# Int8 product of a post-norm decoder moved, in steps, between the quads of its second cross attention

## Chip, core and metric

The kernel runs as one program on one NeuronCore of a Trainium2 chip. The metric is the device time of one execution in microseconds (us). It was run three times, and one more execution was recorded by the hardware profiler. PE is the tensor engine, DVE the vector engine, ACT the scalar engine, POOL the GpSimd engine, and SP the engine that issues most DMAs.

## What is computed

Sixteen sequences of 100 tokens with 256 channels pass through two decoder layers. Each sublayer is followed by an addition and a layernorm. The change touches the last two sublayers only, which are, cut to what matters:

```python
# second cross attention: 16 heads of 64, context of 361 rows with 192 channels
q, k, v = x @ Wq, context @ Wk, context @ Wv
attn = softmax(q @ k.T / 8)
x = layernorm(x + attn @ v @ Wo + bo)

# int8 product with a 256 x 256 right side
lhs_scale = max(abs(x), axis=channels) / 127          # one for each token
rhs_scale = max(abs(rhs), axis=rows) / 127            # one for each column
q_lhs = clip(round(x / lhs_scale), -127, 127)
q_rhs = clip(round(rhs / rhs_scale), -127, 127)
out = layernorm(x + (q_lhs @ q_rhs) * lhs_scale * rhs_scale)
```

The rounded values are whole numbers up to 127 and are held as bf16 for the matmul; the rest of the kernel computes in fp32.

## The kernel before

The 16 sequences stand in four groups of four (`G = 4`, `NG = 4`); `self.x[g]` is a tile of 100 tokens x 4 sequences x 256 channels. The sublayers run one after the other. The last two are the function `cross1` and, behind it in a pool of its own, `quantize_rhs` and four calls of `int8_product`, each followed by the DMA of its group to the output (L1807 to L1811).

**The second cross attention** goes over 64 quads: quad n handles four of the 16 heads of sequence b = n // 4. `attend` (L544) writes the order of PE, ACT and DVE by hand; POOL and SP are ordered by the planner from the order of the program. For each n it issues, in this order:

- `scores(b, quad)`: four score products on PE into two double PSUM banks (L1634), two reduces for the row maximum on DVE (`top`, L1639), four exponentials with row sums on ACT (L1644);
- interleaved, `prepare(b + 1, quad)` and `values` of quad n - 2. The first projects keys (PE L599 and L601, copied out by DVE as `k`, L1598) and, in quads 1 to 3 of a sequence, sources (copied out by DVE as `v`, L1615). The second transposes the probabilities on PE in three tiles (L608), copies them out (`pT`, L611, the first tile on DVE, the other two on ACT), multiplies them by the sources (PE L1673) and copies the result out on ACT (`oT`, L1679);
- `weigh(b, quad)`: a reciprocal of the row sums on DVE (`den`, L1652) and, on POOL, the product of the probabilities with it (L1653);
- at two quads behind the last one of a sequence, so at n % 4 == 1, `finish(b)`: the output projection on PE (16 instructions of L155) and the addition to the residual row on DVE (L1690). For the last sequence of a group, `finish` also calls `close` (L539): the whole layernorm of four sequences, that is eight short DVE instructions for the statistics (L185, L186), a square root on ACT (L192), a reciprocal (L198) and four normalizing instructions on DVE (L200).

`attend` has a parameter `done`, whose steps would go to later quads; `cross1` doesn't use it. PE, ACT and DVE each work through their instructions strictly in this order. PSUM tiles come from three rings of two buffers: `tr` for everything transposed and for the value products, `mm` for projections, `sc` for the scores. An engine that wants a buffer waits until the tile two places earlier in that ring is read out.

**The int8 stage** is not ordered by hand. `quantize_rhs` (L1697) loads the right side, transposes it, takes the scales (L1735 to L1737), rounds by adding and subtracting a large constant (L1715, L1716), clips, turns it back as bf16 and spreads the column scales over the tokens with a matmul (L1725). `int8_product` (L1740) does the like for one group: maximum, scale and inverse (L1735 to L1737), four times scale and round (L1745), two clips over the whole tile (L1748, L1750), eight bf16 transposes (L1755) with two copies on ACT (L1758), eight bf16 matmuls (L155), four times the two scales on DVE (L1770), the addition of x on POOL (L1774) and a layernorm.

Of the kernel before, what the change touches and what calls it, by code (L numbers as in the profile page):

```python
# [90 lines left out]
class Net:  # L91
# [449 lines left out]
        self.x[g] = r  # L541


    def attend(self, scores, prepare, values, finish, queries, weigh, depth, done=lambda g: []):  # L544

        n_quads = 4 * B
        engines = {mybir.EngineType.PE, mybir.EngineType.Activation, mybir.EngineType.DVE}
        with self.tc.manual_schedule(engines=engines):  # L550
            queries(0)
            for part in range(4):
                for step in prepare(0, part):
                    step()
            later = {}
            for n in range(n_quads + depth):
                b, quad = divmod(n, 4)
                ahead, behind = [], []
# [4 lines left out]
                if n >= depth:  # L563
                    behind = values(*divmod(n - depth, 4))
                for i in range(max(len(ahead), len(behind))):
                    for steps in (ahead, behind):
                        if i < len(steps):
                            steps[i]()
                if n < n_quads:
                    weigh(b, quad)  # L570
                if n < n_quads and quad == 2 and b % G == G - 1 and b + 1 < B:
                    queries(b // G + 1)
                for step in later.pop(n, []):
                    step()
                if n >= depth and (n - depth) % 4 == 3:
                    b = (n - depth) // 4
                    finish(b)
                    if b % G == G - 1:

                        for i, step in enumerate(done(b // G)):  # L580
                            later.setdefault(n + 2 * i + 2, []).append(step)
            for n in sorted(later):
                for step in later[n]:
                    step()

    def load_context(self, pool, b):
# [973 lines left out]
    def cross1(self, pool):  # L1560
# [3 lines left out]

        def queries(g):
            x = self.x[g]
            xT = pool.tile([P, 2, GT], F32, tag="xT", name="xT")
            self.transposed(x, xT)

            qTs[g] = []  # L1570
            for i in range(8):
                pq = self.ps("mm")
                self.mm(
                    pq[:, :GT],
                    [(self.x1["wq"][:, k, i * P : (i + 1) * P], xT[:, k, :]) for k in range(2)],
                )
# [120 lines left out]
    def quantize_rhs(self, pool):  # L1697

        nc, small = self.nc, self.small
        raw = pool.tile([P, 2, C], F32, tag="rhs_raw", bufs=1, name="rhs_raw")  # L1700
        nc.sync.dma_start(raw, self.a["rhs"].rearrange("(k p) n -> p k n", p=P))
        self.ident16 = pool.tile([P, P], BF16, tag="ident16", bufs=1, name="ident16")
        nc.vector.tensor_copy(self.ident16, self.c("ident"))
        self.rhs_q = pool.tile([P, 2, C], BF16, tag="rhs_q", bufs=1, name="rhs_q")
        self.rhs_s = pool.tile([T, C], F32, tag="rhs_s", bufs=1, name="rhs_s")
        ps_s = self.ps("mm")
        for o in range(2):
# [10 lines left out]
            nc.vector.tensor_scalar(q16, q, -127.0, None, ALU.max)  # L1718
            pb = self.psum.tile([P, 2, P], BF16, tag="tr", name="tr16")
# [3 lines left out]
            wide = pool.tile([P, T], F32, tag="rhs_wide", bufs=1, name="rhs_wide")  # L1723
            nc.vector.tensor_scalar(wide, self.ones[:, :T], scale, None, ALU.mult)
            nc.tensor.matmul(  # L1725
                ps_s[:T, o * P : (o + 1) * P], wide, self.c("ident"), start=True, stop=True
            )
        nc.scalar.copy(self.rhs_s, ps_s[:T, :C])

    def scales(self, src, rows, n):  # L1730

# [5 lines left out]
        nc.vector.reciprocal(inv, scale)  # L1737
        return scale, inv

    def int8_product(self, pool, g):  # L1740
        nc, x = self.nc, self.x[g]
        scale, inv = self.scales(x, T, G)
        q = pool.tile([T, G, C], F32, tag="q", name="q")
        for b in range(G):
            nc.vector.tensor_scalar(  # L1745
                q[:, b, :], x[:, b, :], inv[:, b : b + 1], MAGIC, ALU.mult, ALU.add
            )
        nc.vector.tensor_scalar(q, q, MAGIC, 127.0, ALU.subtract, ALU.min)  # L1748
        q16 = pool.tile([T, G, C], BF16, tag="q16", name="q16")
        nc.vector.tensor_scalar(q16, q, -127.0, None, ALU.max)  # L1750
        qT = pool.tile([P, 2, GT], BF16, tag="qT16", name="qT16")
        for k in range(2):
            pt = self.psum.tile([P, G, T], BF16, tag="tr", name="tr16")
            for b in range(G):
                nc.tensor.transpose(  # L1755
                    pt[:, b, :], q16[:, b, k * P : (k + 1) * P], self.ident16[:T, :T]
                )
            nc.scalar.copy(qT[:, k, :].rearrange("p (b t) -> p b t", b=G), pt)  # L1758
        r = self.xp.tile([T, G, C], F32, tag="x", name="r")
        for h in range(2):  # L1760
            po = self.ps("mm")
            for b in range(2):
                at = (2 * h + b) * T
                self.mm(
                    po[:T, b * C : (b + 1) * C],
                    [(qT[:, k, at : at + T], self.rhs_q[:, k, :]) for k in range(2)],
                )
            for b in range(2):
                bb = 2 * h + b
                nc.vector.scalar_tensor_tensor(  # L1770
                    r[:, bb, :], po[:T, b * C : (b + 1) * C], scale[:, bb : bb + 1], self.rhs_s,
                    ALU.mult, ALU.mult,
                )
        nc.gpsimd.tensor_tensor(r, r, x, ALU.add)  # L1774
        self.layernorm(r)
        self.x[g] = r


@with_exitstack
def tile_decoder(ctx: ExitStack, tc: tile.TileContext, a: dict, out: bass.AP):  # L1780
# [17 lines left out]
    with tc.tile_pool(name="w_x1", bufs=1, side="right") as wp:  # L1798
        with tc.tile_pool(name="w_out", bufs=1) as w_out:
            net.load_mamba_out(w_out)  # L1800
            net.load_cross1(wp)
            with tc.tile_pool(name="mamba", bufs=2) as pool:
                net.mamba(pool)
        w_in.release()
        with tc.tile_pool(name="cross1", bufs=2) as pool:
            net.cross1(pool)
# [144 lines left out]
```

## Time and profile before

| what | us |
|---|---|
| three runs, median (lowest to highest) | 2077.32 (2067.65 to 2079.21) |
| the profiled execution, its own time | 2075.14 |
| its span, from the first to the last instruction | 2073.4 |
| PE busy over the span | 1813.3 |
| DVE busy over the span | 1120.9 |
| ACT busy over the span | 961.7 |
| POOL busy over the span | 690.1 |
| mean granted clock of PE over the span | 0.932 |
| the row of the last sequence is added (L1690) from | 2015.57 |
| last normalizing instruction of the kernel ends | 2068.1 |

How to read the views: the page of a profile divides the span into 40 slices, 51.8 us each, with the busy share of each engine in tenths. The windows view gives busy time in stretches that one chooses: stretch, its length, then for PE, weight loads (PEld), DVE, ACT and POOL the busy time and the number of instructions, then the granted PE clock (1.00 is full), the share of the DMA engines and GB/s. The timeline lists single instructions: start, duration, engine, line, operation, output and inputs, shapes, and in brackets the idle time of that engine just before and what ended it. "x4" stands for four instructions put together. Matmuls of fp32 count as two instructions each.

### The profile page before, as it was taken

What the parts mean: (1) busy time and instruction counts of PE and PEld (TensorE: products, weight loads), DVE (VectorE), ACT (ScalarE), POOL (GpSimd) and SP (SyncE); (2) the same over time, 40 slices, a digit from 0 to 9 for tenths busy, and PEclk for the clock granted to TensorE, in tenths of its full rate; (3) what the DMA queues carried; (4) which work ended last, traced back from release to release, by engine and by line L of the source; (5) the groups of instructions that cost most, each with busy time, mean ns of one, the idle gap of its engine ahead of it and who ended that gap; (6) DMA issues with size and microseconds to landing.
All of it is one profiled execution on the core that took longest, in us unless ns stands there. A gap on an engine that the chain in (4) does not pass through costs nothing. (4 is left out here: it accounts for less than half of the span.)

```text
span 2073.4 us, 31998 instructions
## 1 busy us (share of the span) xinstructions
PE 1813.3 (87%) x12268; PEld 1066.0 (51%) x12268; DVE 1120.9 (54%) x2458; ACT 961.7 (46%) x2266; POOL 690.1 (33%) x501
## 2 busy tenths in 40 slices
PE   6997999999939994699798899899999999999972
PEld 3565555555626663355455555445545554555551
DVE  3445576667632222587878867444344434434437
ACT  4552476667512221476676676333343334333341
POOL 2222232324320002366667566422223222322221
PEclk9999999999769998699999999999999999999995
DMA  4700600101051114211111111000000000000001
GB/s 130 312 1 1 222 23 16 33 22 32 6 177 44 46 43 143 66 51 53 45 46 60 44 51 38 15 16 8 8 8 15 8 8 8 16 8 8 1 6 32
DMA packets 46840, 96.99 MB, mean 47 GB/s; under 512 B 5835, under 2 KB 25931, under 8 KB 44257
## 3 DMA queue, kind: packets, MB, share of 16 engines
q1 hardware_dynamic: 41632, 83.75, 11.9%
q0 software_dynamic: 5056, 11.20, 1.8%
q8 instruction: 98, 1.61, 0.3%
q14 instruction: 54, 0.43, 0.1%
HBM read 69.48 MB, written 25.44 MB: 46 GB/s over the span
## 5 line engine op out<-in xcount | busy, mean ns | idle before, releaser
L1653 POOL TENSOR_TENSOR s<-s,den 100x1444 f32<-100x1444 f32 x64 | 165.9, 2593 | 513.3 <-DVE den L1652 513.3
L155 PE MATMUL mm<-xT,w_mamba_in 128*128 128x400 f32 x512 | 205.1, 545 | 31.0 <-ACT sz L1344 27.6
L1644 ACT ACTIVATE s<-sc,top 100x361 f32<-100x361 f32 x256 | 140.2, 560 | 158.4 <-DVE top L1639 158.3
L1639 DVE TENSOR_REDUCE top<-sc 100x2 f32<-100x722 f32 x128 | 110.4, 903 | 131.2 <-PE sc L1634 131.2
L611 ACT COPY pT<-tr 128x400 f32<-128x400 f32 (+1 forms) x192 | 94.0, 492 | 182.0 <-PE tr L608 181.8
L753 ACT ACTIVATE w_experts<-w_experts,top 100x361 f32<-100x361 f32 x256 | 149.3, 586 | 41.3 <-POOL w_experts L745 41.1
L1195 DVE SCALAR_TENSOR_TENSOR xc<-mm,pv,xc 128x388 f32<-128x388 f32 (+2 forms) x192 | 119.9, 624 | 80.6 <-ACT xc L1190 75.7
L745 POOL TENSOR_SCALAR w_experts<-w_experts 100x1444 f32<-100x1444 f32 x64 | 88.8, 1388 | 223.1 <-DVE w_experts L741 154.8
L155 PEld LDWEIGHTS mm<-xT,w_mamba_in 128*128 128x128 f32 x512 | 100.7, 205 | 116.0 <-ACT sz L1344 35.2
L611 DVE COPY pT<-tr 128x400 f32<-128x400 f32 x192 | 105.1, 568 | 99.7 <-PE tr L608 66.7
L741 DVE TENSOR_SCALAR_CACHE_REDUCE w_experts<-sc 100x361 f32<-100x361 f32 x256 | 121.0, 528 | 10.6 <-PE sc L735 9.0
L1615 DVE COPY v<-mm 128x512 f32<-128x512 f32 (+1 forms) x96 | 61.8, 686 | 112.2 <-PE mm L601 112.2
L608 PE MATMUL tr<-cn,w_experts 100*128 100x100 f32 (+1 forms) x768 | 101.4, 270 | 21.1 <-ACT pT L611 12.4
L155 PE MATMUL sc<-w_experts,e_xT 128*128 x256 | 117.6, 603 | 2.1 <-DMA e_x<-rows 2.1
L608 PEld LDWEIGHTS tr<-cn,s 100*128 100x128 f32 (+1 forms) x768 | 74.7, 151 | 84.4 <-issue 66.2
L1378 POOL TENSOR_TENSOR y<-y,sz 128x400 f32<-128x400 f32 x64 | 66.4, 1038 | 143.4 <-DVE y L1375 112.4
L608 PE MATMUL tr<-cn,s 100*128 100x100 f32 (+1 forms) x768 | 97.8, 263 | 13.4 <-DVE pT L611 13.4
L1315 POOL TENSOR_TENSOR L<-L,cols 100x800 f32<-100x800 f32 x64 | 99.9, 1561 | 26.3 <-DMA L<-sums 26.3
L599 PE MATMUL mm<-x_wv,ctx 128*128 128x512 f32 (+1 forms) x192 | 96.1, 624 | 9.2 <-DVE k L1598 9.2
L1144 POOL DMA_INDIRECT e_sum<-rows,slots x32 | 33.0, 1031 | 213.6 <-DMA x_wq<-in_x_wo_dram 204.3
L1598 DVE COPY k<-mm 128x361 f32<-128x361 f32 x128 | 62.4, 529 | 76.4 <-PE mm L601 76.4
L1398 PE MATMUL acc<-y,w_mamba_out 128*128 128x400 f32 x256 | 102.6, 524 | 0.0
(297 smaller groups left out, 3691.3 us busy)
## 6 DMA issues: line engine op xcount, KB each, us to landing
L<-sums SPq DMA_DIRECT2D x64, 312.5 KB
rows<-nothing SPq DMA_DIRECT2D x15, 1024.0 KB
w_experts<-in_moe_w_dram SPq DMA_DIRECT2D x24, 512.0 KB
ctx<-in_ctxT_dram SPq DMA_DIRECT2D x32, 361.0 KB
e_x<-rows SPq DMA_DIRECT2D x32, 128.0 KB
rows<-e_y SPq DMA_DIRECT2D x32, 128.0 KB
w_mamba_in<-in_m_w_in_dram SPq DMA_DIRECT2D x1, 2048.0 KB
w_mamba_in<-in_m_w_in_dram POOLq DMA_DIRECT2D x1, 2048.0 KB, 9.9
```

The costliest lines, as they stand in the source:

```text
L155: self.nc.tensor.matmul(out, lhsT, rhs, start=i == 0, stop=i == len(pairs) - 1)
L599: self.nc.tensor.matmul(out, lhsT, rhs, start=True, stop=False)
L608: self.nc.tensor.transpose(pt[:n, h * T : (h + 1) * T], probs[:, h, k0 : k0 + n], self.ident(T))
L611: evict(pT[:n, k, :], pt[:n, :GT])
L741: nc.vector.tensor_scalar(s[:, h, :], sc[h // 2][:T, h % 2, :CTX], -1e4, 1e4, ALU.max, ALU.min, accum_out=top[:, h : h + 1],)
L753: nc.scalar.activation(s[:, h, :], s[:, h, :], AF.Exp, bias=top[:, h : h + 1], scale=-1.0, accum_out=dens[b][:, hd : hd + 1],)
L1195: nc.vector.scalar_tensor_tensor(a3[:, :, s:], p3[:, :, : T - s], w(k), a3[:, :, s:], ALU.mult, ALU.add)
L1315: nc.gpsimd.tensor_tensor(ls[n], ls[n], bc(c, 3, T), ALU.subtract)
L1398: nc.tensor.matmul(acc[:, c, :GT], self.w_out[:, i, c * P : (c + 1) * P], y, start=i == 0, stop=i == 15)
L1639: nc.vector.tensor_reduce(top[:, 2 * p : 2 * p + 2], sc[p][:T, :, :CTX], AX.X, ALU.max, negate=True)
L1644: nc.scalar.activation(s[:, h, :], sc[h // 2][:T, h % 2, :CTX], AF.Exp, bias=top[:, h : h + 1], accum_out=den[:, h : h + 1],)
L1653: nc.gpsimd.tensor_tensor(s, s, bc(den, 2, CTX), ALU.mult)
```

## The change

The int8 product becomes a list of small steps, and `attend` issues them at the ends of quads. `attend` takes a table `later` from quad number to steps in place of `done`; a step of quad n comes after everything else of quad n, `finish` included, and quads go on after the 66th with nothing but such steps.

- `close` is no longer called from `finish`. Two steps take its place: `means` (statistics and square root) and `normal` (reciprocal and normalizing), one quad apart.
- For groups 0 to 2 the list begins one quad behind the `finish` of the group's last sequence, at n = 18, 34 and 50 (all n % 4 == 2), with one step in each quad: `means`, `normal`, `steps_of` (scales, and rounding L1745), `bounded` (the two clips), `turned(0)`, `turned(1)` (four transposes and a copy each), two `product` steps (four matmuls and two DVE instructions each), `plus` (POOL), `means`, `normal` with the DMA to the output. That is eleven quads.
- The last group is closed in two parts: sequences 12 to 14 from n = 62, and sequence 15 from n = 66. From n = 66 on, both lists have a step at the same n, and that of the first part is issued first.
- `quantize_rhs` becomes four steps, issued in quads 4 to 7. Its load is issued ahead of the attention, and its tiles and those of the product now lie in the pool of the cross attention, in one buffer each; `xT` of the queries has one buffer there instead of two. The spread of the column scales goes through the `tr` ring, in two halves.

Its core:

```diff
-            later = {}
-            for n in range(n_quads + depth):
+            for n in range(max(n_quads + depth, max(later) + 1)):
...
-                for step in later.pop(n, []):
-                    step()
-                if n >= depth and (n - depth) % 4 == 3:
-                    b = (n - depth) // 4
-                    finish(b)
-                    if b % G == G - 1:
-                        for i, step in enumerate(done(b // G)):
-                            later.setdefault(n + 2 * i + 2, []).append(step)
+                if depth <= n < n_quads + depth and (n - depth) % 4 == 3:
+                    finish((n - depth) // 4)
+                for step in later.get(n, []):
                     step()
...
-            xT = pool.tile([P, 2, GT], F32, tag="xT", name="xT")
+            xT = pool.tile([P, 2, GT], F32, tag="xT", bufs=1, name="xT")
...
-            if b % G == G - 1:
-                self.close(rs[g], g)
-        self.attend(scores, prepare, values, finish, queries, weigh, 2)
+        def means(g, bs):
+            mvs[g] = self.means(rs[g], bs)
+            mvs[g] = mvs[g], self.deviations(mvs[g], bs)
+        def normal(g, bs):
+            self.normalize(rs[g], *mvs.pop(g), bs=bs)
+            self.x[g] = rs[g]
+        for i, step in enumerate(self.quantize_rhs(pool)):
+            add(4 + i, step)
+        for g in range(NG):
+            for bs in [(0, 1, 2, 3)] if g + 1 < NG else [(0, 1, 2), (3,)]:
+                n = 4 * (g * G + bs[-1]) + 6
+                steps = [lambda g=g, bs=bs: means(g, bs), lambda g=g, bs=bs: normal(g, bs)]
+                steps += self.int8_product(pool, g, bs, q_rs)
+                for i, step in enumerate(steps):
+                    add(n + i, step)
+        self.attend(scores, prepare, values, finish, queries, weigh, 2, later)
...
+        return [
+            lambda: steps_of(self.x[g]), bounded, lambda: turned(0), lambda: turned(1),
+            *[lambda two=two: product(two) for two in (bs[:2], bs[2:]) if two],
+            plus, means, normal,
+        ]
...
-    with tc.tile_pool(name="int8", bufs=2) as pool:
-        net.quantize_rhs(pool)
-        for g in range(NG):
-            net.int8_product(pool, g)
-            nc.sync.dma_start(out[g * G : (g + 1) * G].rearrange("b t c -> t b c"), net.x[g])
```

The arithmetic of each step is the one described above, cut to the sequences `bs` that it is called for.

More of the change, by code (lines that the diff above doesn't have):

```diff
@@ L541, in close, with attend @@
         self.x[g] = r
-    def attend(self, scores, prepare, values, finish, queries, weigh, depth, done=lambda g: []):
+    def attend(self, scores, prepare, values, finish, queries, weigh, depth, later):
         n_quads = 4 * B
@@ L562, in attend @@
                         ahead = prepare(b + 1, quad)
-                if n >= depth:
+                if depth <= n < n_quads + depth:
                     behind = values(*divmod(n - depth, 4))
@@ L572, in attend @@
                     queries(b // G + 1)
-                for step in later.pop(n, []):
-                    step()
-                if n >= depth and (n - depth) % 4 == 3:
-                    b = (n - depth) // 4
-                    finish(b)
-                    if b % G == G - 1:
-                        for i, step in enumerate(done(b // G)):
-                            later.setdefault(n + 2 * i + 2, []).append(step)
-            for n in sorted(later):
-                for step in later[n]:
+                if depth <= n < n_quads + depth and (n - depth) % 4 == 3:
+                    finish((n - depth) // 4)
+                for step in later.get(n, []):
                     step()
@@ L1690, in finish @@
             nc.vector.tensor_tensor(row, po[:T, :C], row, ALU.add)
-            if b % G == G - 1:
-                self.close(rs[g], g)
-        self.attend(scores, prepare, values, finish, queries, weigh, 2)
+        mvs, q_rs = {}, {}
+        def means(g, bs):
[4 more added lines that the diff above has]
+            self.x[g] = rs[g]
+        later = {}
+        add = lambda n, step: later.setdefault(n, []).append(step)
+        for i, step in enumerate(self.quantize_rhs(pool)):
[8 more added lines that the diff above has]
+        self.attend(scores, prepare, values, finish, queries, weigh, 2, later)
     def quantize_rhs(self, pool):
@@ L1702, in quantize_rhs, with quantized @@
         self.ident16 = pool.tile([P, P], BF16, tag="ident16", bufs=1, name="ident16")
-        nc.vector.tensor_copy(self.ident16, self.c("ident"))
         self.rhs_q = pool.tile([P, 2, C], BF16, tag="rhs_q", bufs=1, name="rhs_q")
         self.rhs_s = pool.tile([T, C], F32, tag="rhs_s", bufs=1, name="rhs_s")
-        ps_s = self.ps("mm")
-        for o in range(2):
+        d = {}
+        def quantized(o):
+            if o == 0:
+                nc.vector.tensor_copy(self.ident16, self.c("ident"))
             pt = self.ps("tr")
@@ L1718, in quantize_rhs, with turned @@
             nc.vector.tensor_scalar(q16, q, -127.0, None, ALU.max)
+            wide = pool.tile([P, T], F32, tag="rhs_wide", bufs=1, name="rhs_wide")
+            nc.vector.tensor_scalar(wide, self.ones[:, :T], scale, None, ALU.mult)
+            d[o] = q16, wide
+        def turned(o):
+            q16, wide = d.pop(o)
             pb = self.psum.tile([P, 2, P], BF16, tag="tr", name="tr16")
@@ L1722, in quantize_rhs @@
             nc.scalar.copy(self.rhs_q[:, :, o * P : (o + 1) * P], pb)
[L1723 to L1728, printed above, removed]
+            pw = self.ps("tr")
+            nc.tensor.matmul(pw[:T, :P], wide, self.c("ident"), start=True, stop=True)
+            nc.scalar.copy(self.rhs_s[:, o * P : (o + 1) * P], pw[:T, :P])
+        return [lambda f=f, o=o: f(o) for o in range(2) for f in (quantized, turned)]
     def scales(self, src, rows, n):
@@ L1738, in scales @@
         return scale, inv
[L1740 to L1746, printed above, removed]
-            )
[L1748 to L1756, printed above, removed]
-                )
[L1758 to L1769, printed above, removed]
@@ new lines, in int8_product, with steps_of, bounded, turned @@
+    def int8_product(self, pool, g, bs, rs):
+        nc, nb = self.nc, len(bs)
+        at, cols = slice(bs[0], bs[-1] + 1), slice(bs[0] * T, (bs[-1] + 1) * T)
+        d = {}
+        def steps_of(x):
+            d["scale"], inv = self.scales(x[:, at], T, nb)
+            q = d["q"] = pool.tile([T, G, C], F32, tag="q8", bufs=1, name="q8")
+            for i, b in enumerate(bs):
+                nc.vector.tensor_scalar(
+                    q[:, b, :], x[:, b, :], inv[:, i : i + 1], MAGIC, ALU.mult, ALU.add
+                )
+        def bounded():
+            q = d["q"]
+            nc.vector.tensor_scalar(q[:, at], q[:, at], MAGIC, 127.0, ALU.subtract, ALU.min)
+            d["q16"] = pool.tile([T, G, C], BF16, tag="q16", bufs=1, name="q16")
+            nc.vector.tensor_scalar(d["q16"][:, at], q[:, at], -127.0, None, ALU.max)
+        def turned(k):
+            if k == 0:
+                d["qT"] = pool.tile([P, 2, GT], BF16, tag="qT16", bufs=1, name="qT16")
+            pt = self.psum.tile([P, G, T], BF16, tag="tr", name="tr16")
+            for b in bs:
+                nc.tensor.transpose(
+                    pt[:, b, :], d["q16"][:, b, k * P : (k + 1) * P], self.ident16[:T, :T]
+                )
+            nc.scalar.copy(
+                d["qT"][:, k, cols].rearrange("p (b t) -> p b t", b=nb), pt[:, at]
+            )
+        def product(two):
+            if two[0] == 0:
+                rs[g] = self.xp.tile([T, G, C], F32, tag="x", name="r")
+            po, r = self.ps("mm"), rs[g]
+            for i, b in enumerate(two):
+                self.mm(
+                    po[:T, i * C : (i + 1) * C],
+                    [(d["qT"][:, k, b * T : (b + 1) * T], self.rhs_q[:, k, :]) for k in range(2)],
+                )
+            for i, b in enumerate(two):
+                j = b - bs[0]
@@ L1770, in int8_product, with plus @@
                 nc.vector.scalar_tensor_tensor(
-                    r[:, bb, :], po[:T, b * C : (b + 1) * C], scale[:, bb : bb + 1], self.rhs_s,
+                    r[:, b, :], po[:T, i * C : (i + 1) * C], d["scale"][:, j : j + 1], self.rhs_s,
                     ALU.mult, ALU.mult,
                 )
-        nc.gpsimd.tensor_tensor(r, r, x, ALU.add)
-        self.layernorm(r)
-        self.x[g] = r
+        def plus():
+            r = rs[g]
+            nc.gpsimd.tensor_tensor(r[:, at], r[:, at], self.x[g][:, at], ALU.add)
@@ new lines, in means, with normal @@
+        def means():
+            mv = self.means(rs[g], bs)
+            d["mv"] = mv, self.deviations(mv, bs)
+        def normal():
+            r = rs[g]
+            self.normalize(r, *d["mv"], bs=bs)
+            b0 = g * G
+            nc.sync.dma_start(
+                self.out[b0 + bs[0] : b0 + bs[-1] + 1].rearrange("b t c -> t b c"), r[:, at]
+            )
+        return [
[3 more added lines that the diff above has]
+        ]
@@ L1805, in tile_decoder @@
         with tc.tile_pool(name="cross1", bufs=2) as pool:
+            net.out = out
             net.cross1(pool)
-    with tc.tile_pool(name="int8", bufs=2) as pool:
-        net.quantize_rhs(pool)
-        for g in range(NG):
-            net.int8_product(pool, g)
-            nc.sync.dma_start(out[g * G : (g + 1) * G].rearrange("b t c -> t b c"), net.x[g])
     net.psum.release()
```

## The prediction

> **What bounds the kernel now.** First the windows view: a plain sequence of four quads, one in which a group is closed, the end of the attention, and the stretch from the last residual row to the end.
>
> ```profile
> 1573.79:1612.57 38.78, 37.72 (x250) 20.62 (x249) 17.35 (x31) 14.36 (x44) 10.37 (x5) 1.00 0.04 10
> ...
> 1702.20:1745.07 42.87, 39.58 (x250) 20.99 (x249) 20.72 (x44) 17.11 (x47) 10.37 (x5) 0.96 0.03 9
> ...
> 1989.97:2015.99 26.02, 21.57 (x193) 15.34 (x192) 6.76 (x13) 10.99 (x30) 6.46 (x3) 1.00 0.00 1
> 2015.99:2073.40 57.41, 14.01 (x76) 9.31 (x76) 45.96 (x133) 6.15 (x16) 10.04 (x4) 0.54 0.12 34
> ```
>
> A plain sequence is bound by PE (37.72 of 38.78 us); DVE is busy for 17.35 us. The last stretch, 57.4 us, is bound by DVE (45.96), and PE does 14.01 at half clock. The change spreads most of that DVE work over stretches where DVE has room. A closing costs 42.87 - 38.78 = 4.09 now; the timeline tells how:
>
> ```profile
> 1709.00 1.38 DVE L200 TENSOR_SCALAR x_row<-x_row,ln_mv,ln_rstd 100x256 f32<-100x256 f32 x4
> ...
> 1710.30 1.72 DVE L1639 TENSOR_REDUCE top<-sc 100x2 f32<-100x722 f32 x2
> 1711.28 1.28 ACT L1644 ACT_TABLE_LOAD   x1 [2.52 <-DVE top L1639]
> 1711.94 0.96 DVE L1598 COPY k<-mm 128x361 f32<-128x361 f32 x2
> 1712.51 0.30 PEld L599 LDWEIGHTS mm<-x_wv,ctx 128*128 128x128 f32 x2 [2.43 <-DVE k L1598]
> 1712.51 3.06 PE L599 MATMUL mm<-x_wv,ctx 128*128 128x512 f32 x4 [2.24 <-DVE k L1598]
> 1712.57 0.56 ACT L1644 ACTIVATE s<-sc,top 100x361 f32<-100x361 f32 x1
> ```
>
> The layernorm stands before `top` on DVE, so `k` is late and PE waits 2.24. The other 1.85 is the clock: after the wait it was 0.66 for 4 us, and the sources took 3.06 instead of 1.93. So DVE's slack where one quad ends and the next begins (call it a seam) is what counts. Timeline, a plain seam:
>
> ```profile
> 1585.93 0.17 DVE L1652 RECIPROCAL den<-den 100x4 f32<-100x4 f32 x1
> 1586.24 2.59 POOL L1653 TENSOR_TENSOR s<-s,den 100x1444 f32<-100x1444 f32 x1 [10.35 <-DVE den L1652]
> ...
> 1587.56 1.73 DVE L1639 TENSOR_REDUCE top<-sc 100x2 f32<-100x722 f32 x2 [1.46 <-PE sc L1634]
> ...
> 1590.37 0.98 DVE L1598 COPY k<-mm 128x361 f32<-128x361 f32 x2 [1.08 <-PE mm L601]
> ```
>
> A step lands between `den` and `top`. DVE idles 1.46 there and 1.08 before `k`: 2.5 us are free, and each further one holds PE. After the first quad of a sequence (n % 4 == 0) it is 2.91 + 1.08 = 4.0; after `finish` (n % 4 == 1) 0.37 + 1.08 = 1.45. But POOL starts its 2.59 right after `den`. What that does to DVE, in the last stretch (a tiny instruction, normally 0.14) and as the attention starts:
>
> ```profile
> 2034.10 2.72 POOL L1774 TENSOR_TENSOR r<-r,x_row 100x1024 f32<-100x1024 f32 x1 [27.50 <-DVE r L1770]
> 2034.53 2.31 DVE L1736 TENSOR_SCALAR q_scale<-q_scale 100x4 f32<-100x4 f32 x1
> ```
>
> ```profile
> 1321.35 0.39 DVE L185 BATCH_NORM_STATS2 ln_st<-r 100x6 f32<-100x256 f32 x1
> ...
> 1323.07 3.14 DVE L200 TENSOR_SCALAR r<-r,ln_mv,ln_rstd 100x256 f32<-100x256 f32 x4
> ```
>
> A TENSOR_SCALAR from SBUF to SBUF is held until POOL is done (3.14 instead of 1.38 beside POOL's L207, 1320.43 to 1325.09); the statistics are not (0.39 beside it), nor is `top`, which reads PSUM.
>
> **The change, part by part.** Sums are made against the profiled span of 2073.4; the execution took 2075.14, 1.7 more and 2.2 below the median of the three runs.
>
> *Tail, -36.4.* The old one, from the end of the last L1690 (2015.99), is 57.4. The new one, with that end as zero: clips of three sequences, 2 x 0.68 x 3/4 = 1.0; transposes and copy (0.53 + 0.50, three of four sequences) to 1.9; ACT then loads the square root table for sequence 15 (1.28 + 0.30) before the second copy: 4.0; first product 1.0, two L1770 of 0.42: 5.8; sequence 15's scales (1.1) stand before the third L1770: 7.3; POOL 2.34 x 3/4: 9.1; a clip of 0.3 held by it and statistics 3 x 0.55: 11.1; root, reciprocal, three L200: 12.7. Then sequence 15: its L1770 13.1, POOL 0.6, statistics 0.55, root 0.4, reciprocal and L200 0.5: 15.4; output and end as now, 2073.4 - 2068.1 = 5.3: 20.7, say 21. 57.4 - 21 = 36.4. Both ends: if every second wait overlaps better 18, if each POOL and table wait doubles 26.
>
> *Groups 0 to 2, +2.3 each, +6.9.*
> - The closing leaves `finish`: -4.09.
> - PE work: 8 transposes (0.85) and 8 matmuls (1.94) at clock 0.50; at 1.00 half of it: +1.4. All on the path, as PE is the bound.
> - `means` (n % 4 == 2): 2.21 of statistics from `den`, under 2.5: 0. ACT loads two tables more (1.28 each); exponentials come 2.0 late, but in a quad with sources the second `pT` copy (1591.26) is needed only when the value products start (1594.43): 3 to spare.
> - `normal` (n % 4 == 3): L200 is held by POOL until 2.6 after `den`, then 1.0 to 1.4: ends 3.9 after it, 1.4 over 2.5. +1.4; with PE's usual 0.7 gap there it is a gap like the 2.24 above, so +1.5 for clock (bounds 0 and 1.85).
> - `steps_of` (n % 4 == 0): reduce 1.21, L1736 held until POOL ends, reciprocal, four L1745 of 0.33: 0.5 over. The trace has no such reduce beside POOL; bounds 0 (not held, nothing late) and 1.7 (held); I take 0.5, as the statistics of the nearest row were not held.
> - `bounded`, after `finish`: POOL is idle by then, 1.3 against 1.45: 0. `turned`, `product`: DVE's two L1770 read PSUM, ACT's copy (0.45) fits its 1.46 of idle: 0 beyond PE. `plus`: POOL has 5 us idle in each quad: 0; without that cover the probabilities, due two quads later, still come in time. The outputs go through SP between loads of contexts that are issued once in four quads: 0.
> - second `means` (n % 4 == 3): exponentials 2.0 late (0.75 from `top`, 1.28 table) before a quad without sources, where the copies (1600.54 for products at 1601.69) have only 1.0 with ACT's own idle 0.42: +1.0, and +0.5 for clock. second `normal`: +0.1.
> - Sum: 1.4 + 1.4 + 1.5 + 0.5 + 1.0 + 0.5 + 0.1 - 4.09 = 2.3.
>
> The Trainium skill, "ScalarE: Activation LUTs", section "What ACT_TABLE_LOAD costs", puts a drain of 1.38 behind each load of 1.28 and so speaks against four loads in place of two. The row above differs: the exponential starts 1.29 after its load. By the page the second `means` would cost 1.4 more in each group, 4 us in all; I go by the row.
>
> The Trainium skill, "SBUF — State Buffer", section "Who interferes with whom", says that a `tensor_reduce` never contends with GpSimd on this chip. By it `steps_of` keeps its 0.5; were the reduce held, the sum would be 3.6 higher. No run here shows it yet.
>
> *Right side, quads 4 to 7, +4.1.* PE work L1710, L1721, L1725, 3.06 in the tail at mostly half clock: +1.7. At n = 4 DVE ends 0.35 over; at n = 6 L1736 waits for POOL and the rest takes 1.6 more: 1.55 over; clock +0.5. The load, now early on SP, is due 36 us after the attention starts; xT's single buffer is free since the group before: 0. Bounds 1.7 and 7.3.
>
> *Last group inside the loop, +4.0.* From n = 62 no projections run and the quads hang on the chain score, `top`, exponential, copy (5.86 each, 1993.53 to 1999.39). `means` at 62 puts a table load into it: +1.4. `normal` at 63 waits for POOL ahead of a `pT` copy: +1.75. Clock +0.85. `steps_of` ends 0.3 before the next `pT`: 0; without that cover up to 1.
>
> Sum: -36.4 + 6.9 + 4.1 + 4.0 = -21.4: span 2052.0, time 2053.7, so **2054 us**.
>
> **Rivals.**
> - *Steps hide.* DVE's TENSOR_SCALARs get in ahead of POOL (0.14 lies between the end of `den` and POOL's start). Then a group costs 1.4 + 1.0 + 0.5 - 4.09 = -1.2, the right side 1.7, the last group 1.4: -36.4 - 3.6 + 3.1 = -36.9, time **2038**. Against it: L1736 at 2034.53 was held although other DVE work preceded it. 0.2.
> - *Every stall drops the clock.* 1.85 for `normal`, `means` and `steps_of` of each group: 5.8 a group, 17.4; right side 7.3, last group 6.9: -36.4 + 31.6 = -4.8, time **2070**, within 0.5%. Against it: quads with gaps of 0.87 and 0.84 (2002.6 and 2004.0) ran at 1.00; for it: like gaps at 1980.5 and 1981.9 were followed by 0.79. 0.14, mostly between 2062 and 2070.
> - *Slower.* One mechanism: at the seams all DVE instructions, not TENSOR_SCALAR alone, wait for POOL, and PE with them. 29 steps in the loop use DVE (8 in each of three groups, 2, 3). The gains are 36.4 + 12.3 = 48.7, PE work takes 5.9 of it; above 42.8 / 29 = 1.5 a step it turns, and at the full 2.59 it is 75: **2107**. Against it: `top` takes 1.73 beside POOL. 0.04.
>
> **How the numbers follow.** Forecast 0.62 (2045 to 2062), the rivals 0.20, 0.14 and 0.04. About 0.5% is what a measurement of this kernel can tell from no change; 0.5% below 2075.1 is 2064.8. Faster: 0.62 + 0.20 + 0.06 of the clock rival = 0.88; same 0.08; slower 0.04. The range 2037 to 2066 leaves out some 0.07 below and 0.12 above.
>
> **What would show it.** From the last L1690 to the end: 21 (18 to 26) instead of 57.4. Sequences that close a group: some 39 where they take 42.87, and the next two longer than 38.78 by 6 together, at the seams with `normal` (L200 of some 3 us beside L1653) and the second `means`. L1736 of some 2 us in quads 4, 6 and in `steps_of`. Wrong would be: a tail over 30, L200 beside POOL at 0.34 each, or waits of PE for the `mm` or `tr` ring behind the new transposes and products.

## Result and the profile after

| what | before, us | after, us |
|---|---|---|
| median of the runs beside each other (lowest to highest, 4 each) | 2075.24 (2067.65 to 2079.21) | 2052.21 (2048.37 to 2053.87) |
| the profiled execution / its span | 2075.14 / 2073.4 | 2053.87 / 2052.1 |
| PE, DVE, ACT, POOL busy over the span | 1813.3, 1120.9, 961.7, 690.1 | 1815.1, 1140.3, 971.6, 690.4 |

The ratio is 0.9892, with a 95% interval of 0.9876 to 0.9908. The time forecast was 2054, and the changed kernel is faster by about the amount foretold, though not for quite the reasons foretold.

The changed kernel's lines are numbered a little differently: `top` is L1631, the exponential L1636, `den` L1644, POOL's product L1645, the score matmul L1626, the transposes L600, `pT` L603, the value products L1665, the residual row L1682, and of the int8 part the scales L1754 to L1756, rounding L1769, clips L1775 and L1777, turning L1784 and L1787, product L1802, addition L1809.

As before, stretches run from one residual row to the next. A plain sequence is one into which no step falls (38.78). "Second statistics" and "second closing" are the `means` and the pair of `means` and `normal` of the layernorm behind the int8 product. The windows view of the kernel after: the sequence in which group 0 is closed, the two behind it, the last two sequences and the tail.

```profile
1539.85:1581.35 41.50, 39.36 (x250) 21.21 (x252) 26.90 (x52) 17.02 (x47) 10.38 (x4) 0.96 0.03 10
1581.35:1621.25 39.90, 38.85 (x262) 21.61 (x263) 19.34 (x35) 15.14 (x46) 12.70 (x5) 1.00 0.04 10
1621.25:1661.13 39.88, 38.27 (x254) 20.89 (x254) 23.76 (x46) 16.92 (x47) 12.72 (x5) 1.00 0.07 21
...
1963.98:2003.15 39.17, 33.96 (x230) 20.02 (x230) 20.71 (x40) 16.83 (x47) 12.72 (x5) 0.91 0.04 12
2003.15:2031.30 28.15, 22.62 (x176) 17.25 (x176) 13.74 (x29) 12.26 (x31) 5.19 (x2) 0.76 0.00 1
2031.30:2052.10 20.80, 3.31 (x16) 1.73 (x16) 10.69 (x30) 3.25 (x8) 2.52 (x2) 0.57 0.07 20
```

The tail fell from 57.41 to 20.80. The closing sequence fell from 42.83 to 41.50, while the two behind it rose by 1.1 each. The last two sequences rose from 34.81 and 21.93 to 39.17 and 27.73 (from row to row), at a clock of 0.91 and 0.76. So the gain is the tail, and a good part of the price is paid at the end of the loop. In full:

| stretch | before | after | difference |
|---|---|---|---|
| up to the attention's first matmul | 1321.89 | 1324.00 | +2.1 |
| from there to the first residual row (after: with the first step of the right side, from 1396.01) | 84.33 | 85.53 | +1.2 |
| sequence 1 (right side) | 38.77 | 40.68 | +1.9 |
| group 0 closed, and the two sequences with its int8 steps | 42.83, 38.77, 38.78 | 41.50, 39.90, 39.88 | +0.9 |
| group 1, the same | 42.87, 38.77, 38.78 | 41.19, 39.90, 39.87 | +0.5 |
| group 2 closed, and the sequence behind it | 42.92, 38.77 | 40.26, 39.90 | -1.5 |
| last two sequences | 34.81, 21.93 | 39.17, 27.73 | +10.2 |
| tail | 57.41 | 20.80 | -36.6 |
| span (other stretches: 0.0) | 2073.4 | 2052.1 | -21.3 |

Now single places. The timeline of the kernel after, at the seam where group 0 is normalized (the answer to the row of 1709.00 before):

```profile
1557.59 0.17 DVE L1644 RECIPROCAL den<-den 100x4 f32<-100x4 f32 x1
1557.85 3.75 DVE L200 TENSOR_SCALAR x_row<-x_row,ln_mv,ln_rstd 100x256 f32<-100x256 f32 x4
1557.90 2.59 POOL L1645 TENSOR_TENSOR s<-s,den 100x1444 f32<-100x1444 f32 x1 [6.67 <-DVE ln_rstd L198]
1561.53 1.71 DVE L1631 TENSOR_REDUCE top<-sc 100x2 f32<-100x722 f32 x2
...
1564.66 0.61 PE L600 MATMUL tr<-cn,s 100*105 100x100 f32 x4 [1.83 <-DVE pT L603]
1565.00 1.19 DVE L1754 TENSOR_REDUCE q_scale<-x_row 100x4 f32<-100x1024 f32 x1
1565.23 2.60 POOL L1645 TENSOR_TENSOR s<-s,den 100x1444 f32<-100x1444 f32 x1 [4.73 <-DVE den L1644]
1566.22 1.62 DVE L1755 TENSOR_SCALAR q_scale<-q_scale 100x4 f32<-100x4 f32 x1
```

The four L200 took 3.75 instead of 1.38, as POOL's L1645 ran from 1557.90 to 1560.49. `top` came 3.9 after `den`, as foretold. PE then had a gap of 1.83, in a place where a plain sequence has one of 0.71, as the timeline of the kernel before shows:

```profile
1601.15 0.61 PE L608 MATMUL tr<-cn,s 100*105 100x100 f32 x4 [0.71 <-DVE pT L611]
```

One quad later the reduce took 1.19 beside POOL (1565.23 to 1567.83), so it isn't held; the tiny L1755 behind it was, for 1.62.

The timeline of the kernel after at the end, ACT's loads and PE's two long gaps, and the tail:

```profile
1985.31 1.28 ACT L1636 ACT_TABLE_LOAD   x1 [0.37 <-DVE top L1631]
1986.59 0.61 PE L600 MATMUL tr<-cn,s 100*105 100x100 f32 x4 [1.40 <-DVE pT L603]
1986.61 0.56 ACT L1636 ACTIVATE s<-sc,top 100x361 f32<-100x361 f32 x1
1989.20 3.78 DVE L200 TENSOR_SCALAR r<-r,ln_mv,ln_rstd 100x256 f32<-100x256 f32 x4
1989.32 1.85 PE L1665 MATMUL tr<-pT,v 128*64 128x100 f32 x24 [2.12 <-ACT pT L603]
...
2010.96 1.28 ACT L1636 ACT_TABLE_LOAD   x1
2014.97 2.27 PE L1665 MATMUL tr<-pT,v 128*64 128x100 f32 x24 [2.29 <-ACT pT L603]
...
2033.19 1.28 ACT L192 ACT_TABLE_LOAD   x1
2038.64 1.79 DVE L1777 TENSOR_SCALAR q<-q 100x256 bf16<-100x256 f32 x1
```

The first load for an exponential (1985.31) waits until `top` is there; the second (2010.96) follows at once on the root, whose own load ran from 2009.36. Both times the `pT` copies stand behind the exponentials on ACT, and PE, which has no projections left to fill with, waits 2.12 and 2.29. In the tail, the load ahead of sequence 15's root and the clip held by POOL (1.79) are the two waits that the sum for the tail had in it.

### What sets PE's clock

The prediction had to guess what a gap does to the clock. The traces answer a good part of it. During the attention, the clock was 0.50 for stretches of 3.41, 6.83 or 13.65 us in each of them, and within a trace all their edges lie on one grid of 3.413 us. A half period, below, is one such period at clock 0.50. The windows view of the kernel after, cut along that grid, at the gap of 1.83 in group 0 and then at the same gap (1.82) in group 2:

```profile
1559.84:1563.25 3.41, 2.99 (x16) 1.56 (x16) 3.41 (x7) 0.73 (x3) 0.65 (x1) 1.00 0.00 0
1563.25:1566.67 3.42, 1.96 (x28) 1.53 (x28) 3.09 (x6) 2.43 (x8) 1.44 (x1) 1.00 0.00 0
1566.67:1570.08 3.41, 3.41 (x13) 1.50 (x10) 3.34 (x8) 0.33 (x1) 1.15 (x1) 0.50 0.02 5
1570.08:1573.49 3.41, 3.41 (x18) 1.86 (x17) 2.24 (x4) 2.78 (x9) 0.00 (x0) 1.00 0.01 2
```

```profile
1904.58:1908.00 3.42, 2.23 (x14) 1.02 (x13) 3.42 (x8) 1.51 (x5) 0.00 (x0) 1.00 0.00 0
1908.00:1911.41 3.41, 2.73 (x34) 2.01 (x36) 3.08 (x5) 1.98 (x7) 2.21 (x1) 1.00 0.00 0
```

In group 0, 1.46 of one period were idle (3.42 - 1.96), and the whole next period ran at half clock, 2 us after the gap had ended. In group 2 the edge cut the gap in two: 1.19 and 0.68 were idle, and the clock stayed. Counted over the attention in all ten traces (the two kernels and the eight below): of some 1980 periods at full clock, none with less than 1.25 of PE idle was followed by a half one, two of the ten between 1.25 and 1.43 were, and all 45 above 1.43 were. A period at half clock costs at most 1.7, half of 3.41: closing sequences of the changed kernel took 40.26 with none behind the gap, 41.19 and 41.50 with one, and in e5 42.78 with two. The grid stands differently to the work from one kernel and one group to the next, so the same code pays or doesn't. The cost of a gap is a chance, which rises with its length. What holds the clock down for a second period is in part open: all 7 half periods with 0.75 or more idle were followed by another, but so were 6 of the 63 with under 0.31.

The Trainium skill, "TensorE: Matmul & The Clock Gate", section "What's actually happening", gives a free-running window of 4096 cycles, 3413 ns; the traces agree. Its table lets the clock fall after an idle window; here more than 1.43 idle of 3.41 was always enough, and 1.31 was in e4.

### The profile page after: what moved, and what is told of

Same layout as the page of the kernel before. It is cut to its first block, busy times and chain, and to the rows that moved or that the text cites. A ratio compares the mean times of both kernels' runs of the same rounds, so it can differ in the third digit from the quotient of the medians.

```text
span 2052.1 us, 31981 instructions
## 1 busy us (share of the span) xinstructions
PE 1815.1 (88%) x12268; PEld 1070.4 (52%) x12268; DVE 1140.3 (56%) x2465; ACT 971.6 (47%) x2279; POOL 690.4 (34%) x502
## 5 line engine op out<-in xcount | busy, mean ns | idle before, releaser
L1645 POOL TENSOR_TENSOR s<-s,den 100x1444 f32<-100x1444 f32 x64 | 166.0, 2594 | 506.3 <-DVE den L1644 465.4
L1636 ACT ACTIVATE s<-sc,top 100x361 f32<-100x361 f32 x256 | 140.3, 561 | 182.6 <-DVE top L1631 174.6
L603 ACT COPY pT<-tr 128x400 f32<-128x400 f32 (+1 forms) x192 | 94.0, 494 | 167.1 <-PE tr L600 165.3
L603 DVE COPY pT<-tr 128x400 f32<-128x400 f32 x192 | 105.1, 568 | 96.9 <-PE tr L600 63.7
L1631 DVE TENSOR_REDUCE top<-sc 100x2 f32<-100x722 f32 x128 | 110.1, 901 | 87.1 <-PE sc L1626 87.1
L600 PEld LDWEIGHTS tr<-cn,s 100*128 100x128 f32 (+1 forms) x768 | 76.2, 154 | 87.2 <-issue 63.9
L600 PE MATMUL tr<-cn,w_experts 100*128 100x100 f32 (+1 forms) x768 | 101.3, 270 | 21.1 <-ACT pT L603 12.4
L600 PE MATMUL tr<-cn,s 100*128 100x100 f32 (+1 forms) x768 | 99.4, 267 | 17.2 <-DVE pT L603 17.0
L1665 PE MATMUL tr<-pT,v 128*64 128x100 f32 (+1 forms) x1536 | 98.2, 268 | 12.1 <-ACT pT L603 7.3
L600 PEld LDWEIGHTS tr<-cn,w_experts 100*128 100x128 f32 (+1 forms) x768 | 79.5, 157 | 42.4 <-issue 25.8
```

The lines of the kernel that those rows point to most:

```text
L600: self.nc.tensor.transpose(pt[:n, h * T : (h + 1) * T], probs[:, h, k0 : k0 + n], self.ident(T))
L603: evict(pT[:n, k, :], pt[:n, :GT])
L1631: nc.vector.tensor_reduce(top[:, 2 * p : 2 * p + 2], sc[p][:T, :, :CTX], AX.X, ALU.max, negate=True)
L1636: nc.scalar.activation(s[:, h, :], sc[h // 2][:T, h % 2, :CTX], AF.Exp, bias=top[:, h : h + 1], accum_out=den[:, h : h + 1],)
L1645: nc.gpsimd.tensor_tensor(s, s, bc(den, 2, CTX), ALU.mult)
L1665: nc.tensor.matmul(po[64 * jj : 64 * jj + 64, i * T : (i + 1) * T], v[k][:n, (4 * quad + h) * 64 : (4 * quad + h + 1) * 64], pT[:n, k, h * ...
```

## Experiments

**Theory:** beside the tail, the price paid in the loop is set by three things: PE's own added work, the normalizing instructions that POOL holds at a seam, and the table loads where ACT is on the path (second statistics, last sequences). **Rivals:** the gain comes from splitting the closing alone; the last group's second list in the loop is the culprit, not the loads; the price is bad luck of the clock. Each run's median stands with its ratio to the kernel before, run beside it (median 2073.33 for e1 to e4, 2074.22 for e5 to e8), and the 95% interval of that ratio; a run has four executions, e3 ten and e6 five. Times of single sequences are from one profiled execution of each. "Stretch" is from the attention's first matmul to the end of the span (751.5 before, 728.1 after), because the start itself varied from 1316.19 to 1324.00 between the runs.

**e1, the root without a square root table.**

```diff
-            mvs[g] = mvs[g], self.deviations(mvs[g], bs)     # Sqrt on ACT, reciprocal on DVE
+            mvs[g] = mvs[g], self.inverse_root(mvs[g], bs)
+        self.nc.scalar.activation(rstd[:, at], mv[:, at, 1], AF.Ln, bias=self.eps[:T])
+        self.nc.scalar.activation(rstd[:, at], rstd[:, at], AF.Exp, scale=-0.5)
```

> The inverse root of the seven closings in the last two sublayers is exp(-0.5 ln(var + eps)) instead of a square root and a reciprocal, so that ACT may keep one table that holds both exp and ln. Theory: beside the tail, what the change costs comes from two things at the seams, DVE's normalizing held by POOL, and ACT's table loads ahead of the exponentials, which hurt most in the last sequence, where no projection covers them and PE's clock falls to 0.5 behind the gaps. With the loads gone, the last two sequences (27.7 and 39.2 us between the last three residual rows, before 21.9 and 34.8) lose 6 to 8 us, the second statistics of groups 0 and 1 lose 0.5 each, and the tail loses 1.5: 2052 to about 2043. The seam with the normalizing step keeps its 2.7. Rival: ACT has idle time enough, the loads are hidden, and DVE alone causes the gaps: only the tail moves, 2050 to 2051.

2048.07 (0.9877, 0.9861 to 0.9894), stretch 726.5. The loads did not go; the timeline of e1, in its tail:

```profile
2026.47 1.28 ACT L207 ACT_TABLE_LOAD   x1
2027.76 0.29 ACT L207 ACTIVATE ln_rstd<-ln_mv,eps 100x1 f32<-100x1 f32 x1
2028.07 1.28 ACT L208 ACT_TABLE_LOAD   x1
2029.37 0.20 ACT L208 ACTIVATE ln_rstd<-ln_rstd 100x1 f32<-100x1 f32 x1
```

Logarithm and exponential loaded a table each, so the premise fell, and the tail rose by 3.1. But in the loop the exponential's table is now loaded straight behind the logarithm and no longer waits for `top`: the second statistics cost 0.5 less (39.88 to 39.36; e5, without any load, came to 39.21), the last two sequences 2.2 and 1.6 less. So at the second statistics it counts less how many loads there are than whether one stands behind `top`.

**e2, the steps ahead of `den`, so that POOL is idle while they run.**

```diff
                 if n < n_quads:
+                    for step in later.get(n, []):
+                        step()
                     weigh(b, quad)
...
-                for step in later.get(n, []):
-                    step()
+                if n >= n_quads:
+                    for step in later.get(n, []):
+                        step()
```

> In quads below 64 the step is issued ahead of the quad's reciprocal, so that POOL's multiplication starts only behind it and cannot hold the step's TENSOR_SCALARs. Nothing else moves. Theory (DVE is held by POOL): the four normalizing instructions take 1.4 instead of 3.8 us, the seam with them no longer stalls PE, and its clock stays at 1.00: 2.7 less in each of groups 0 and 1, 2 to 3 less in the last two sequences: about 2044. Rival (the lock is beside the point, DVE is simply too full at the seams, whichever engine runs): at most 1 us less, 2051 to 2052. It could even cost: POOL starts later by the step's length, but the probabilities are due two quads later.

2045.75 (0.9872, 0.9856 to 0.9889), stretch 720.6. The timeline of e2 at the normalizing seam:

```profile
1554.58 1.38 DVE L200 TENSOR_SCALAR x_row<-x_row,ln_mv,ln_rstd 100x256 f32<-100x256 f32 x4
1555.88 0.17 DVE L1647 RECIPROCAL den<-den 100x4 f32<-100x4 f32 x1
1556.00 1.73 DVE L1634 TENSOR_REDUCE top<-sc 100x2 f32<-100x722 f32 x2
1556.19 2.59 POOL L1648 TENSOR_TENSOR s<-s,den 100x1444 f32<-100x1444 f32 x1 [6.06 <-DVE den L1647]
```

L200 takes 1.38 again, and all three closing sequences take 38.77 or 38.78, what a plain one takes. Here the whole closing, statistics and normalizing, is free. As at this seam only the order against `den`, and with it POOL's start, differs, POOL's hold was the price there. The last two sequences, from which 2 to 3 had been expected, stay nearly as they were (38.62 and 27.60 against 39.17 and 27.73).

**e3, only the closings split** (the kernel before, with `means` at n % 4 == 2 and `normal` one quad later; the int8 stage at the end, as before).

```diff
+        for g in range(NG):
+            n = 4 * (g * G + 3) + 6
+            later[n] = [lambda g=g: means(g)]
+            later[n + 1] = [lambda g=g: normal(g)]
+        self.attend(scores, prepare, values, finish, queries, weigh, 2, later)
```

> The kernel before, with nothing but its four layernorms behind the attention taken out of the residual step and cut into statistics and normalizing, one quad apart; the right side and the int8 product stay in the tail. Theory: the tail keeps some 57 us, each of three closings costs 2.7 (seam with POOL, and clock) instead of 4.1: 3 to 5 us less than before, about 2071. Rival: closings split in two hide wholly, 12 us less than before, 2063; then a good part of the change's gain is theirs and not the tail's.

2073.07 against 2073.33 (0.9995, 0.9985 to 1.0005), stretch 747.4, tail 57.51. Closings took 41.38, 41.49 and 39.90. The rival's 12 falls, and the theory's 3 to 5 doesn't show in the times either, though in the profiled execution, the second fastest of the ten (2070.33), the stretch is 4.1 shorter than before. So the gain is the tail's. The three closings hold the same instructions and the same gap of 1.83; the last one alone met no half period. The windows view of e3 there:

```profile
1874.39:1914.29 39.90, 37.75 (x250) 20.61 (x252) 22.94 (x44) 17.01 (x47) 10.37 (x4) 1.00 0.04 10
```

PE is busy as in a plain sequence (37.75), at full clock, and 1.1 go to the gap alone.

**e4, the last group in one piece.**

```diff
-            for bs in [(0, 1, 2, 3)] if g + 1 < NG else [(0, 1, 2), (3,)]:
+            for bs in [(0, 1, 2, 3)]:
```

> The changed kernel with the last group closed in one piece, its list starting behind the last residual row. Theory: the part of three sequences costs 5.8 us inside the loop (statistics and normalizing at quads 62 and 63, and the clock behind them), and takes 5 to 6 us off the tail: closed in one piece the stretch between the last two residual rows falls from 27.7 to 21.9 and the tail grows from 20.8 to 26: 2052 within 1. Rival: the two parts are what makes the tail short at no cost in the loop: 2057 to 2058.

2053.36 (0.9899, 0.9882 to 0.9917), stretch 730.7. The last sequence fell from 27.73 to 24.37 (foretold 21.9; two half periods fell into it), the tail rose from 20.80 to 24.69 (foretold 26): two parts or one are the same within what can be told. Sequence 14, the last but one, stayed at 39.17, so the first part isn't its culprit; group 2's second closing has a share in it (e7). Up to there e4 has the code of the kernel after, and yet one of its sequences with second statistics took 41.26 instead of 39.88. The grid again, the windows view of e4 and then of the kernel after at that seam:

```profile
1641.88:1645.29 3.41, 2.10 (x32) 1.64 (x32) 2.51 (x5) 2.40 (x9) 1.40 (x1) 1.00 0.00 0
1645.29:1648.71 3.42, 3.42 (x10) 1.49 (x11) 3.42 (x6) 0.52 (x2) 1.19 (x1) 0.50 0.05 15
```

```profile
1641.76:1645.17 3.41, 2.92 (x16) 1.49 (x15) 2.86 (x5) 3.02 (x8) 0.58 (x1) 1.00 0.00 0
1645.17:1648.59 3.42, 2.60 (x34) 2.02 (x36) 2.51 (x4) 2.10 (x7) 2.04 (x1) 1.00 0.02 5
```

Gaps of 0.71 and 0.60 fell into one period in e4 (1.31 idle), and into two in the other.

**e5, no root at all.** It leaves the square root out of the closings that the change touches (a linear function in its place), so that no table changes.

```diff
+        self.nc.scalar.activation(rstd[:, at], mv[:, at, 1], AF.Identity, bias=self.eps[:T])
```

> The changed kernel without the square root in the seven closings of the last two sublayers (ACT copies the variance instead), so that ACT keeps its exponential table; the output differs by that. Theory: in the last two sequences (39.2 and 27.7 us between the last three residual rows, 34.8 and 21.9 before the change) most of the extra 10 us is ACT's table loads ahead of the exponentials, plus PE's clock falling behind those gaps: they fall to about 36.5 and 24. The second statistics of groups 0 and 1 lose their 0.5, the tail 1.3 to 1.6. The seam with the normalizing step keeps its 2.7. In all 8 us less than the changed kernel, about 2044. Rival (the gaps there are DVE's, held by POOL, as in the other groups): the loads cover no more than 1 us each in two places, 2049 to 2050.

2043.50 (0.9852, 0.9836 to 0.9867), stretch 721.3. The last two sequences took 36.45 and 24.91, 2.7 and 2.8 less than after; second statistics 39.21 instead of 39.88; the tail 19.02, 1.8 less. So, in these two executions, the loads were worth about 5.5 of the 10.2 at the end of the loop, and their clock is in that: two half periods there, where the kernel after has six.

**e7, group 2 through earlier** (its eleven steps in ten quads, so that its last ones end one quad sooner), and **e8, the first part of the last group from n = 64**, ahead of `finish`, with the second part's later steps pushed behind it:

```diff
+                at = (0, 1, 2, 3, 4, 4, 5, 6, 6, 8, 9) if g == 2 else range(len(steps))    # e7
+                n += 2 if bs == (0, 1, 2) else 0                                          # e8
+                at = (0, 1, 2, 3, 6, 7, 8, 9, 10, 11) if bs == (3,) else range(len(steps))  # e8
```

> The changed kernel with group 2's eleven steps in ten quads, so that its second closing ends at quad 59 and no longer lies in the last sequence's first quads, which have no projections. Theory: a table load before a quad with sources is covered, before a quad without projections it is not: 39.2 falls to 36 or 37, the rest stays: 2 to 3 us less, about 2049. Rival (place in the sequence doesn't matter): within 1 of the changed kernel, 2052, the cost only moving one sequence forward.

> The changed kernel with the part of three sequences two quads later (statistics at quad 64, behind the last exponential), its normalizing issued ahead of the last residual row. No exponential table is then needed again. Theory: the stretch between the last two residual rows falls from 27.7 to 22 to 24, the tail grows by 1 to 3: 2 to 3 us less, about 2049. Rival (clock and gaps there come from group 2's closing before it): the stretch stays over 26 and the tail grows: 2053 to 2054.

e7: 2051.10 (0.9896, 0.9880 to 0.9913), stretch 727.4, not below the 0.9892 of the kernel after, where 2 to 3 us less had been expected. Sequence 14 fell from 39.17 to 37.65, but the one ahead of it rose from 39.90 to 40.67: half of what was gained there only moved. e8: 2049.02 (0.9881, 0.9865 to 0.9898), stretch 726.7. The last sequence fell from 27.73 to 23.77 with the tail at 21.08. So 4.0 of the 5.8 in that sequence came from the place of the first part's steps, whose statistics and normalizing had stood where PE hangs on ACT; the clock is in that, one half period there instead of four. Two other sequences with unchanged code met a half period (41.25 instead of 39.88, 41.43 instead of 40.26), and took 2.5 of it back. The interval of e8's ratio, too, overlaps that of the kernel after (0.9876 to 0.9908): the gain stands in the sequences, not in the time.

**e6, what helped, together:** the steps ahead of `den` (e2), e7 and e8, and a tiny exponential behind each root of groups 0 to 2, so that the load of the exponential's table no longer waits for `top` (from e1).

```diff
+            one = small.tile([T, 1], F32, tag="one", name="one")
+            nc.scalar.activation(one, self.eps[:T], AF.Exp)
```

> Steps ahead of the reciprocal at every quad; a tiny exponential behind each square root inside the loop, which loads the exponential table before the row maximum is there; group 2's list shortened by putting two steps in one quad, so that it ends before the last sequence's quads; the last group's part of three sequences two quads later, behind the last exponential. Theory: closings cost 38.8 a sequence as plain ones, second closings hide, the last two sequences fall to 35 and 22 to 23, the tail stays within 2 of 20.8: 15 us less than the changed kernel, about 2037. Rival (the seams are not what costs; the time goes with PE's added work): no better than the variant with steps ahead of the reciprocal, 2044 to 2046.

2036.97 (0.9818, 0.9804 to 0.9832), stretch 713.5: it beats both kernels. The timeline and then the windows view of e6 (a closing, the last two sequences, the tail):

```profile
1548.77 0.30 ACT L192 ACTIVATE ln_rstd<-ln_mv,eps 100x4 f32<-100x4 f32 x1
1549.08 1.28 ACT L1694 ACT_TABLE_LOAD   x1
1550.38 0.20 ACT L1694 ACTIVATE one<-eps 100x1 f32<-100x1 f32 x1
1550.49 0.55 ACT L1636 ACTIVATE s<-sc,top 100x361 f32<-100x361 f32 x1
```

```profile
1537.81:1576.59 38.78, 37.73 (x250) 20.62 (x252) 24.58 (x54) 17.20 (x48) 10.37 (x4) 1.00 0.04 11
...
1954.99:1990.40 35.41, 31.81 (x226) 18.93 (x228) 17.60 (x38) 16.79 (x48) 10.37 (x4) 0.95 0.05 13
1990.40:2013.99 23.59, 19.25 (x176) 14.07 (x176) 9.08 (x21) 10.75 (x30) 5.19 (x2) 0.93 0.00 1
2014.41:2035.50 21.09, 3.40 (x16) 1.95 (x16) 11.36 (x37) 1.98 (x7) 2.52 (x2) 0.58 0.07 20
```

The exponential's load now follows at once on the root, where the kernel after let 0.37 pass until `top` was there (1985.31). No run has the tiny exponential by itself; beside e2, it took the sequences with second statistics from 39.18 to 38.92. The end of the loop costs 2.3 over the kernel before (35.41 + 23.59 against 34.81 + 21.93), where the kernel after paid 10.2, and the tail's gain is kept. From the attention's start to the last row it had three half periods; the kernel after had ten, the one before five.

## Why the prediction held, and where it did not

That the forecast of the span, 2052.0, met 2052.1 so closely is luck, as errors cancelled: the change's price in the loop was put at 15.0 and came out at 12.4 (1.9 + 0.4 + 0.9 + 0.5 - 1.5 + 10.2), while 2.9 came from elsewhere (2.1 before the attention, and 0.8 of clock at its start). Besides, the profiled execution is the slowest of the four (2053.87; median 2052.21).

- **Tail, -36.4:** right, -36.6, with both of the waits named; the last normalizing instruction ended 15.2 behind the row, foretold 15.4. (The pieces of that sum, as written, add up to a few tenths less than its 20.7.)
- **Closing leaves `finish`, -4.09:** right; e2 shows the whole of it gained. *PE work +1.4:* 1.7 (busy time of 38.85 and 38.27 over a plain 37.72: 1.13 + 0.55).
- **`normal`, +1.4 and +1.5 for the clock:** the mechanism was right: 3.75 for L200, a gap 1.13 longer than usual. Closing sequences came to 2.7, 2.4 and 1.5 over a plain one; the last met no half period, so the clock was 1.2, 0.9 and 0. The sign given for it, closings at some 39 and the next two sequences longer by 6 together, put this seam a sequence too late: it lies before the next residual row, and the two behind it grew by 2.2.
- **`steps_of`, +0.5:** 0.4, the closing sequence of group 2 (40.26) against e3's (39.90), both at full clock, which differ by this step. The reduce isn't held; L1755 is. The Trainium skill, "SBUF — State Buffer", section "Who interferes with whom", on `tensor_reduce` agrees with the 1.19 beside POOL.
- **Second `means`, +1.0 and +0.5 for the clock:** 39.88 is 1.1 over a plain sequence, of which 0.55 is PE work; so some 0.5, and in this trace no clock. The exponential starts 1.30 after its load (1985.31 to 1986.61), and in e6 the load of 1549.08 stands between two activations without a gap; so the drain of 1.38 that the Trainium skill ("ScalarE: Activation LUTs", "What ACT_TABLE_LOAD costs") adds to a load isn't in these traces, and the row was the right guide.
- **Groups, +2.3 each:** +0.9 and +0.5 for the two that lie wholly in full quads; too dear by 1.4 to 1.8. Without the clock the terms give -0.4 now and gave +0.3 then; the rest is the clock, put at 2.0.
- **Right side, +4.1:** +2.3, that is +1.9 in sequence 1, of which PE's work is 1.6 (busy for 39.34 over a plain 37.72), and 0.4 for the first step, which runs before the first residual row. Its term that failed is "at n = 6 L1736 waits for POOL". In the timeline of the kernel after, while POOL ran from 1418.67 to 1421.26:

```profile
1420.03 0.15 DVE L1755 TENSOR_SCALAR q_scale<-q_scale 128x1 f32<-128x1 f32 x1
...
1420.93 0.48 DVE L1730 TENSOR_SCALAR rhs_t<-rhs_t 128x256 f32<-128x256 f32 x1
```

  With one element in each partition it took 0.15, as at 1396.95, beside POOL too; the row it was priced by had four (2.31). L1730 behind it was held, but only for some 0.2 (0.48 against 0.29 for L1716 in the tail before), as POOL was nearly done.
- **Last group, +4.0:** this is the step that failed. The last two sequences rose by 10.2, of which only about 2.2 had been booked elsewhere (group 2's second `product`, 0.55, and second closing, 1.6). The table load had been put at +1.4 and the normalizing at +1.75, each once; but group 2's second closing hangs on the same chain from the quads without projections on (1985 to 1990), and it was priced like one in a full quad. The clock had been put at +0.85; there were six half periods instead of one. e5 puts the loads at 5.5, e8 the first part's place at 4.0; they overlap, and how the rise divides between loads, hold and clock stays open.
- **Before the attention, +2.1, and its first stretch, +1.2:** no part of the change runs in the first but the load and the order of tiles, and its end varied by 7.8 between kernels, with the early load both in the earliest (e7) and in the latest; the cause stays open. In the second, the attention of the kernel after starts with 3.7 us at half clock, that of the one before with 2.3. e3, which has no right side there and starts with 3.8 at half clock, took 85.12, 0.8 more than before; the remaining 0.4 is the right side's first step.
- **Rivals:** the steps don't hide as they stand, but e2's do, and its groups and closings then came to -2.1 (foretold -1.2). "Every stall drops the clock" was half right: which stalls do is counted above. Nothing spoke for slower: `top` (1.73 beside POOL in e2) and the reduce (1.19) weren't held.

## What to carry over

Put work of DVE that reads and writes SBUF ahead of the instruction that releases POOL, not behind it: the same four instructions cost 1.38 or 3.75. Where ACT changes tables, make it change back while it is idle (a tiny activation did it here, for 0.26 in a sequence), and keep such steps out of quads in which the bound engine has nothing else to fill with. Price a gap of PE by its length and by a chance of a period at half clock, not by one observed drop, and compare kernels by stretches, since that chance fell differently in groups and kernels with the same code.

## What had not been expected of the hardware

- PE's clock goes by a grid of periods of 3.413 that stands anywhere to the work (counted above), so one gap of 1.83 had three prices: none, one or two half periods.
- The 128x1 TENSOR_SCALAR wasn't held beside POOL (0.15, twice), the 100x4 one was (1.62, three times).
- Ln and Exp in turn loaded a table each time (1.28 each, 2026.47 and 2028.07 in e1).
- A load for an exponential waits with the exponential for its input: in the kernel before, ACT idled for 2.52 ahead of the load of 1711.28, until `top` came.
